# Patch writes paced at one per slot, six shared patch buffers, and a re-ordered start in a convolution kernel that TensorE bounds

## The chip, the cores and the metric

One core of a Trainium2 chip. The metric is the device time of one execution in microseconds (us). The 22 or 23 executions of the kernel before in a set of rounds spread over 0.8 to 1.1% (3105.9 to 3141.0 us at the widest). The record marks every execution here as undisturbed ("fast"). A change counts as faster or slower when it moves the time by over 2%, here 62 us.

## The reference, cut to what matters

For each of 16 images of 256 channels and 28 x 28 pixels: a group normalization, two 3x3 convolutions in which each channel's nine-pixel patch is replaced by a softmax over 16 centroids, each followed by a batch norm, then a squeeze-and-excite gate and two residual additions.

```python
def amm_conv3x3(x, centroids, w_sub, stride=1):
    patches = jax.lax.conv_general_dilated_patches(x, (3, 3), (stride, stride), 'SAME')
    p = patches.reshape(B, C, s, Ho * Wo).transpose(0, 3, 1, 2)
    d = jnp.sum(p * p, axis=-1)[..., None] - 2.0 * jnp.einsum('bncs,cks->bnck', p, centroids) + jnp.sum(centroids * centroids, axis=-1)[None, None]
    attn = jax.nn.softmax(-d, axis=-1)
    lut = jnp.einsum('cks,cso->cko', centroids, w_sub)
    out = jnp.einsum('bnck,cko->bno', attn, lut)
...
v = _gn(x)
out = relu(bn(amm_conv3x3(v, centroids1, wsub1)))
out = se_layer(bn(amm_conv3x3(out, centroids2, wsub2)))
return x + relu(out + v)
```

## The kernel before

The program is a plan of slots. A stage is one layer of one image: two pixel tiles (384 and 400 pixels) times eight groups of channels, 16 units, one per slot. I call a stage of layer 1 "L0" and one of layer 2 "L1"; they alternate, 32 in all, numbered 0 to 31. In each slot TensorE makes one unit's logits (L549) from its patches, ScalarE (ACT) takes the exponential (L607), TensorE makes the numerators (L617), VectorE and GpSimd transpose and divide, and TensorE multiplies with the sub-weights three slots later (L681, "looks").

The patches go through DRAM. Twelve writes per image and layer put the shifted image there, issued from ACT's queue, 588 KB each. Each unit then loads its part with four transfers of about 110 KB from SP's queue. In layer 2 four units of a stage are "maxed": their logits are made six slots early, and their maxima go out to DRAM (`dm<-mt`) and come back (`pm<-dm`) by small transfers, also on ACT's queue.

```python
    def to_pat(l, i, pat):                       # one of 12 patch writes
        ...
        nc.scalar.dma_start(
            view(pat, (ROWS * p0 + 9 * k + 3 * dx) * HW, [[ROWS * HW, n], [HW, 3], [1, HW]]),
            bass.AP(v.tensor, v.offset, [list(v.ap[0]), [W, 3], [1, HW]]),
        )
    ...
    def patches(u):                              # the four loads of a unit
        (px, n), mx = u["px"], u["maxed"]
        tiles = pms if mx else pts               # 2 tiles for maxed units, 4 for others
        pt = tiles[loads[mx] % len(tiles)]
        ...
        for i in range(4):
            nc.sync.dma_start(pt[32 * i : 32 * i + ROWS, :, :n], view(u["pat"], ...))
    ...
        def prep(self, l, pat, t, pace):
            for i, dx in enumerate((0, 2)):
                for k in range(NB):
                    self.at(t + i, REST, shift, l, dx, k)
            for i in range(len(STEPS)):
                self.at(t + i // pace, REST, to_pat, l, i, pat)
    ...
        elif l == 0 and b > 1:
            t0 = t - 2 * NS                      # NS = 16
            plan.at(t0, REST, load_x, b, x[b])
            plan.norm(b, t0 + 3)
            plan.prep(0, pat_of(0, b), t0 + 12, 1)
        if l == 1:
            near = b in (0, B - 1)
            plan.prep(1, pat_of(1, b), t - NS + (LC if near else 0), 3 if near else 2)
```

## Time and profile before

| | kernel before |
|---|---|
| time | 3122.45 us, median of 3 runs (3121.16 to 3123.53) |
| span of the profiled run | 3124.6 us |
| TensorE busy | 2951.3 us, mean granted clock 0.974 |
| up to the first numerators | 51.8 us |
| stage 0, stage 1 | 139.6, 129.6 us |
| 13 full L0 stages (3, 5, ... 27) | 1260.8 us, 93.2 to 102.3 each |
| 14 L1 stages (2, 4, ... 28) | 1233.6 us |
| stages 29 and 30 | 90.0 and 99.1 us |

A stage runs from the first numerators of its first slot to those of the next stage. The last stage and the tail together take 119 to 123 us in all kernels here.

The prediction shows PE's side. The other side, which it did not show, is what SP's queue of patch loads waits for. Columns: total us, times, the longest.

```profile
SPq L536 <- PE pair L549: 661.1, 276, 10.7
SPq L536 <- DMA pat<-im: 318.4, 62, 11.0
SPq L536 <- DMA pat<-side: 298.7, 113, 23.6
SPq L536 <- DMA dm<-mt: 283.2, 66, 11.5
```

The first line is the loads' natural pace: a buffer comes free when the logits that read it are done. The other three are loads that wait for a patch write (`pat`) or for a maximum going out (`dm`). In the steady part they have no tie by data to that transfer: the writes then going out are for a later stage.

### The profile page before, as it was taken

Reading aid. Unit: us, or ns where it says so; the run is one execution under the profiler, and the core shown is the slowest. Engines: PE = TensorE matmul, PEld = TensorE weight load, DVE = VectorE, ACT = ScalarE, POOL = GpSimd, SP = SyncE. Lnnn points to the kernel's source line nnn. Section 1 sums busy time; section 2 is a strip of 40 time slices with the busy share of each in tenths; the row PEclk is TensorE's granted clock in tenths of the full one; section 3 lists DMA queues with packets and bytes.
Section 4 is the critical chain, followed back from the end, with each engine's and each line's share of the span. In section 5 each row is a group of like instructions: output and inputs, shape, how many; then the busy total and the mean of one; then the engine's idle time right before and its main releaser. Section 6 shows DMA issues by size and latency. Waiting matters only on the chain. (4 is left out here: it accounts for less than half of the span.)

```text
span 3124.6 us, 94006 instructions
## 1 busy us (share of the span) xinstructions
PE 2951.3 (94%) x39838; PEld 1167.1 (37%) x39838; DVE 2255.7 (72%) x2756; ACT 1094.0 (35%) x1611; POOL 1504.2 (48%) x2165
## 2 busy tenths in 40 slices
PE   3898999999999999999999999999999999999997
PEld 2432333333333333333333333333333333333333
DVE  3364777787777877768787776868777777777785
ACT  1332343333433334343333433333333333334232
POOL 1343455454545545454555545445554454545344
PEclk9998999999999999999999999999999999999998
DMA  7666666665766666567666656766566666656641
GB/s 209 187 165 147 152 197 172 178 171 149 204 171 196 168 179 161 143 195 185 193 166 169 184 145 194 188 187 157 155 182 166 195 164 174 167 146 196 179 103 50
DMA packets 331901, 530.23 MB, mean 170 GB/s; under 512 B 93664, under 2 KB 251088, under 8 KB 331472
## 3 DMA queue, kind: packets, MB, share of 16 engines
q10 hardware_dynamic: 144000, 244.45, 30.2%
q1 hardware_dynamic: 180560, 241.14, 29.1%
q0 software_dynamic: 6912, 38.54, 3.6%
q8 instruction: 316, 5.18, 0.7%
q14 instruction: 113, 0.93, 0.1%
HBM read 269.96 MB, written 254.05 MB: 168 GB/s over the span
## 5 line engine op out<-in xcount | busy, mean ns | idle before, releaser
L681 PE MATMUL acc<-q,ws 128*128 128x384 f32 (+1 forms) x4096 | 1662.4, 525 | 5.3 <-ACT y L703 5.3
L645 POOL TENSOR_TENSOR k<-nt,rc 128x832 f32<-128x832 f32 (+1 forms) x512 | 804.3, 1571 | 1579.6 <-DVE rc L635 1573.6
L629 DVE STREAM_TRANSPOSE nt<-pair 128x832 f32<-128x832 f32 (+1 forms) x1024 | 978.1, 993 | 765.1 <-PE pair L617 625.9
L607 ACT ACTIVATE e<-pair 128x800 f32<-128x800 f32 (+1 forms) x1024 | 787.2, 821 | 1511.1 <-PE pair L549 1251.5
L681 PEld LDWEIGHTS acc<-q,ws 128*128 128x128 f32 x4096 | 704.9, 191 | 917.0 <-issue 595.1
L617 PE MATMUL pair<-e,cw 32*32 32x384 f32 (+1 forms) x16384 | 601.3, 509 | 60.5 <-ACT e L607 60.1
L663 DVE STREAM_TRANSPOSE q<-k 128x832 f32<-128x832 f32 (+1 forms) x512 | 489.2, 956 | 0.8 <-POOL k L645 0.8
L549 PE MATMUL pair<-pt,wd 19*32 19x384 f32 (+1 forms) x14336 | 439.2, 509 | 22.8 <-DMA pt<-pat 22.5
L635 DVE RECIPROCAL rc<-nt 128x104 f32<-128x104 f32 (+1 forms) x512 | 398.7, 779 | 17.6
L617 PEld LDWEIGHTS pair<-e,cw 32*32 32x32 f32 x16384 | 169.7, 103 | 414.0 <-ACT e L607 382.8
L651 POOL TENSOR_TENSOR tail<-nt,rc 128x104 f32<-128x104 f32 (+1 forms) x512 | 244.8, 478 | 0.0
L681 PE MATMUL acc<-qt,ws 128*128 128x400 f32 (+1 forms) x512 | 221.5, 515 | 0.0
L549 PEld LDWEIGHTS pair<-pt,wd 19*32 19x32 f32 x14336 | 107.1, 103 | 285.1 <-issue 210.1
L657 POOL TENSOR_TENSOR total<-total,nt 128x96 f32<-128x96 f32 (+1 forms) x448 | 200.2, 447 | 0.0
L657 POOL TENSOR_TENSOR total<-total,rc 128x96 f32<-128x96 f32 (+1 forms) x448 | 177.8, 397 | 0.0
L549 PE MATMUL pair<-pm,wd 19*32 19x384 f32 (+3 forms) x4096 | 147.4, 502 | 10.7 <-DMA pm<-pat 10.5
L568 DVE STREAM_TRANSPOSE z<-pair 128x768 f32<-128x768 f32 (+1 forms) x128 | 120.3, 978 | 38.4 <-PE pair L549 38.4
L681 PEld LDWEIGHTS acc<-qt,ws 128*128 128x128 f32 x512 | 91.7, 191 | 102.1 <-issue 53.2
L573 DVE TENSOR_REDUCE mx<-z 128x48 f32<-128x768 f32 (+1 forms) x128 | 120.8, 944 | 0.0
L693 ACT ACTIVATE im<-acc,bnsh,bnsc 128x384 f32<-128x384 f32 (+1 forms) x64 | 43.4, 678 | 154.5 <-PE acc L681 154.5
L703 ACT ACTIVATE y<-acc,bnsh,bnsc 128x384 f32<-128x384 f32 (+1 forms) x64 | 43.4, 678 | 91.6 <-PE acc L681 76.3
L549 PEld LDWEIGHTS pair<-pm,wd 19*32 19x32 f32 (+1 forms) x4096 | 34.4, 103 | 104.5 <-issue 65.4
(105 smaller groups left out, 763.1 us busy)
## 6 DMA issues: line engine op xcount, KB each, us to landing
pat<-side ACTq DMA_DIRECT2D x256, 588.0 KB
pt<-pat SPq DMA_DIRECT2D x896, 112.5 KB
pt<-pat SPq DMA_DIRECT2D x896, 108.0 KB
pat<-im ACTq DMA_DIRECT2D x128, 588.0 KB
xt<-in_x POOLq DMA_DIRECT2D x32, 784.0 KB, 9.7
pm<-pat SPq DMA_DIRECT2D x128, 112.5 KB
pm<-pat SPq DMA_DIRECT2D x128, 108.0 KB
out_dram<-y POOLq DMA_DIRECT2D x16, 784.0 KB, 4.5
```

What stands on the lines that cost most here:

```text
L549: nc.tensor.matmul(ps[t // 2][c : c + 32, t % 2, :n], lhsT=wd[l][32 * i : 32 * i + rows, 4 * u["m"] + t, :], rhs=u["pt"][32 * i : 32 * i + ...
L568: nc.vector.transpose(z[:, : 64 * nb].rearrange("p (t m) -> p t m", t=2), ps[:, :, : 32 * nb])
L573: nc.vector.tensor_reduce(u["mx"][:, 2 * v : 2 * v + 2].rearrange("p t (j b) -> p t b j", j=2)[:, :, :nb], u["z"].pop(0)[:, : 64 * nb].rea ...
L607: nc.scalar.activation(e[:, :, :n], ps[:, :, :n], AF.Exp, scale=2.0)
L617: nc.tensor.matmul(u["nm"][t // 2][32 * i : 32 * i + 32, t % 2, :n], lhsT=cw[l][c : c + 32, 4 * u["m"] + t, :], rhs=es[t // 2][c : c + 32, ...
L629: nc.vector.transpose(nt[:, :nb, 2 * v : 2 * v + 2].rearrange("p b t r -> p t b r"), ps[:, :, : 32 * nb].rearrange("p t (b r) -> p t b r", ...
L635: nc.vector.reciprocal(rc[:, : 8 * nb], u["nt"][:, :, SUM])
L645: nc.gpsimd.tensor_tensor(q[:, :nb].rearrange("p b (a s) -> p (b a) s", s=8), nt[:, :, :8], rc.unsqueeze(2).to_broadcast([P, 8 * nb, 8]), ...
L651: nc.gpsimd.tensor_tensor(tails[key][:, :nb, 8 * (m % 4) : 8 * (m % 4) + 8], nt[:, :, 8].rearrange("p (b a) -> p b a", a=8), rc.rearrange( ...
L657: nc.gpsimd.tensor_add(t[:, : 8 * nb], t[:, : 8 * nb], v)
L663: nc.vector.transpose(q[:, :, : 32 * nb].rearrange("p h (b r) -> p h b r", r=32), u.pop("k")[:, :nb].rearrange("p b (h r) -> p h b r", h=2),)
L681: nc.tensor.matmul(accs[key][:, :n], lhsT=ws[l][:, 2 * m + h if h < 2 else 2 * NQ + m // 4, o * P : (o + 1) * P], rhs=u["q"][h][:, :n], st ...
```

## The change

Its intent: take the patch writes of layer 2 from two per slot at the start of an L0 stage to one per slot in L1 stages, so that they stop holding up ACT; share six patch buffers among all units; move the normalization to where the memory is quieter (DMA share 0.58 in the L1 stage that the prediction shows, 0.70 in the L0 stage after it); and shorten the start, by writing and using the first pixel tile first.

```diff
-    pts = [const.tile([P, 4, 400], F32, name=f"pt{i}") for i in range(4)]
-    pms = [const.tile([P, 4, 400], F32, name=f"pm{i}") for i in range(2)]
+    pts = [const.tile([P, 4, 400], F32, name=f"pt{i}") for i in range(6)]
...
         def emit(self):
+            free = [-99] * len(pts)
+            for slot, last, u in sorted(self.loads, key=lambda v: v[:2]):
+                tile = free.index(min(free))
+                assert free[tile] <= slot
+                free[tile] = last
+                self.at(slot, LOAD, patches, u, tile)
...
-                        at(a - self.lead + 1, REST, patches, u)
+                        self.loads.append((a - self.lead, s, u))
...
-        def prep(self, l, pat, t, pace):
+        def prep(self, l, pat, t):
+            for i, dx in enumerate((0, 2)):
+                for k in range(NB):
+                    self.at(t + 4 * i + 2 + k, REST, shift, l, dx, k)
+            for i in range(len(STEPS)):
+                self.at(t + i, REST, to_pat, l, i, pat)
+
+        def prep_near(self, l, pat, t, slots, t2, slots2):     # images 0 and 15
...
+                self.at(t + i * slots // len(STEPS), REST, to_pat, l, i, pat, *PXT[0])
+                self.at(t2 + i * slots2 // len(STEPS), REST, to_pat, l, i, pat, *PXT[1])
...
+        if l == 0 and b >= 1:
+            n0 = -3 if b == 1 else t - 2 * NS - 3
+            plan.at(n0 - 2, REST, load_x, b, x[b])
+            plan.norm(b, n0)
+            plan.prep(0, pat_of(0, b), {1: 1, 2: 32, 3: 56}.get(b, t - 2 * NS + 3))
         if l == 1:
-            plan.prep(1, pat_of(1, b), t - NS + (LC if near else 0), 3 if near else 2)
+            if b in (0, B - 1):
+                t0 = t - NS + LC
+                plan.prep_near(1, pat_of(1, b), t0, 4, t0 + 4, 8)
+            else:
+                plan.prep(1, pat_of(1, b), 44 if b == 1 else t - 2 * NS + LC + 1)
...
-    for i in range(NLT * P // PART):
-        plan.at(i // 3, REST, sort_ws1, i)
+    n1 = NLT * P // PART
+    for i in range(n1):
+        if i < 2:
+            plan.at(-6, REST, load_part, ws1, i)
+            plan.at(-1, REST, sort_ws1, i)
+        else:
+            plan.at((i - 2) * 3 // 4 - 1, REST, load_part, ws1, i)
+            plan.at((i - 2) * 3 // 4, (LOOK_A, LOOK_B)[i % 2], sort_ws1, i)
```

Cut: the second pixel tile of image 0 is written in slots 0 to 3, the second layer's sub-weights are loaded a slot before their sort, the set-up of its codes moves from slot 20 to 15, the squares of the codes go to a function of their own, one of three copies of a sort goes to VectorE, the norm takes six slots instead of eight, and three placing moves per slot replace four.

More of the change, by code (lines that the diff above doesn't have):

```diff
@@ L150 @@
     load_x(0, x[0])
-    pts = [const.tile([P, 4, 400], F32, name=f"pt{i}") for i in range(4)]
-    pms = [const.tile([P, 4, 400], F32, name=f"pm{i}") for i in range(2)]
-    for t in pts + pms:
+    pts = [const.tile([P, 4, 400], F32, name=f"pt{i}") for i in range(6)]
+    for t in pts:
         nc.sync.dma_start(t[ONE::32], view(consts, 0, [[0, 4], [0, 4], [1, 400]]))
@@ L295, with load_part @@
     PART = 384
-    def part_of(ap, i):
+    parts = {}
+    def load_part(ap, i):
         t = tpool.tile([P, 832], F32, tag="z", name="part")[:, : NB * PART].rearrange("p (b m) -> p b m", b=NB)
         nc.sync.dma_start(t, ap[:, i * PART : (i + 1) * PART].rearrange("(b p) m -> p b m", p=P))
-        return t
+        parts[i] = t
     def sort_ws1(i):
-        t = part_of(ws1, i)
+        t = parts.pop(i)
         for j in range(PART // P):
@@ L310, in sort_ws1 @@
                 )
-            nc.scalar.copy(ws[0][:, i * PART // P + j], ps[:, :C])
+            w = ws[0][:, i * PART // P + j]
+            if j == 1:
+                nc.vector.tensor_copy(w, ps[:, :C])
+            else:
+                nc.scalar.copy(w, ps[:, :C])
     d_c2 = [dram.tile([C, K * 9], F32, name=f"dc2{i}") for i in range(2)]
@@ L337, in sort_ws2 @@
     def sort_ws2(i):
-        t = part_of(wsub2, i)
+        t = parts.pop(i)
         ps = pair()
@@ L374, in place_tail, with square_codes @@
         )
+    squares = []
+    def square_codes(l):
+        wf = wd[l].rearrange("p t m -> p (t m)")
+        for c0 in range(0, NT * 32, 384):
+            n = min(384, NT * 32 - c0)
+            sq = tpool.tile([P, 832], F32, tag="z", name="sq")[:, :n]
+            nc.gpsimd.tensor_tensor(sq, wf[:, c0 : c0 + n], wf[:, c0 : c0 + n], ALU.mult)
+            squares.append((c0, n, sq))
     def setup_codes(l):
         wf = wd[l].rearrange("p t m -> p (t m)")
-        for c0 in range(0, NT * 32, 256):
-            sq = tpool.tile([P, 832], F32, tag="z", name="sq")
-            nc.gpsimd.tensor_tensor(sq[:, :256], wf[:, c0 : c0 + 256], wf[:, c0 : c0 + 256], ALU.mult)
+        for c0, n, sq in squares:
             ps = bank()
-            nc.tensor.matmul(ps[:, :256], lhsT=nhalf_sb, rhs=sq[:, :256], start=True, stop=True)
-            nc.vector.tensor_add(wf[:, c0 : c0 + 256], wf[:, c0 : c0 + 256], ps[:, :256])
+            nc.tensor.matmul(ps[:, :n], lhsT=nhalf_sb, rhs=sq, start=True, stop=True)
+            nc.vector.tensor_add(wf[:, c0 : c0 + n], wf[:, c0 : c0 + n], ps[:, :n])
+        squares.clear()
         nc.vector.tensor_add(wd[l], wd[l], mones_sb[:, l].unsqueeze(1).to_broadcast([P, NT, 32]))
@@ L448, with to_pat @@
     STEPS = [(dx, k, h) for dx in (1, 0, 2) for k in range(NB) for h in range(2)]
-    def to_pat(l, i, pat):
+    def to_pat(l, i, pat, px=0, n=HW):
         dx, k, h = STEPS[i]
-        p0, n = P // 2 * h, P // 2
-        v = (ims[l] if dx == 1 else sides[dx])[p0 : p0 + n, k]
+        p0, m = P // 2 * h, P // 2
+        v = (ims[l] if dx == 1 else sides[dx])[p0 : p0 + m, k, px:]
         nc.scalar.dma_start(
-            view(pat, (ROWS * p0 + 9 * k + 3 * dx) * HW, [[ROWS * HW, n], [HW, 3], [1, HW]]),
-            bass.AP(v.tensor, v.offset, [list(v.ap[0]), [W, 3], [1, HW]]),
+            view(pat, (ROWS * p0 + 9 * k + 3 * dx) * HW + px, [[ROWS * HW, m], [HW, 3], [1, n]]),
+            bass.AP(v.tensor, v.offset, [list(v.ap[0]), [W, 3], [1, n]]),
         )
@@ L524, in store, with patches @@
             d.pop(b)
-    loads = {True: 0, False: 0}
-    def patches(u):
-        (px, n), mx = u["px"], u["maxed"]
-        tiles = pms if mx else pts
-        pt = tiles[loads[mx] % len(tiles)]
-        u["mx"] = mxs[loads[mx] % 2]
-        loads[mx] += 1
+    maxed = [0]
+    def patches(u, tile):
+        px, n = u["px"]
+        pt = pts[tile]
+        if u["maxed"]:
+            u["mx"] = mxs[maxed[0] % 2]
+            maxed[0] += 1
         for i in range(4):
@@ L710 @@
     LOOKS = [(m, o, h) for m in range(NQ) for o in range(2) for h in range(3 if m % 4 == 3 else 2)]
-    LOGITS, EXP, LOOK_A, NUM, TURN, SMALL, LOOK_B, MAX, LOOK_C, TURN_BACK, REST = range(11)
+    LOGITS, EXP, LOOK_A, NUM, TURN, SMALL, LOOK_B, MAX, LOOK_C, TURN_BACK, LOAD, REST = range(12)
     class Plan:
@@ L722, in __init__ @@
             self.tiles = []
+            self.loads = []
         def at(self, slot, pos, f, *a):
@@ L761, in stage @@
                     else:
-                        at(s - self.lead, REST, patches, u)
+                        self.loads.append((s - self.lead, s, u))
                     at(s, LOGITS, b_logits, u)
@@ L775, in prep @@
             for i in range(len(STEPS)):
-                self.at(t + i // pace, REST, to_pat, l, i, pat)
+                self.at(t + i * slots // len(STEPS), REST, to_pat, l, i, pat, *PXT[0])
+                self.at(t2 + i * slots2 // len(STEPS), REST, to_pat, l, i, pat, *PXT[1])
         def norm(self, b, t):
             self.at(t, REST, gn_stats, b, 0)
-            self.at(t + 2, REST, gn_stats, b, 1)
-            self.at(t + 4, SMALL, gn_mean, b)
-            self.at(t + 5, SMALL, gn_var, b)
-            self.at(t + 6, REST, gn_apply, b, 0)
-            self.at(t + 7, REST, gn_apply, b, 1)
+            self.at(t + 1, REST, gn_stats, b, 1)
+            self.at(t + 2, SMALL, gn_mean, b)
+            self.at(t + 3, SMALL, gn_var, b)
+            self.at(t + 4, REST, gn_apply, b, 0)
+            self.at(t + 5, REST, gn_apply, b, 1)
         def close(self, b, ob, te, pace):
@@ L815 @@
             shift(0, dx, k)
-        to_pat(0, i, d_pat[0])
+        to_pat(0, i, d_pat[0], *PXT[0])
+    square_codes(0)
     setup_codes(0)
@@ L825 @@
         plan.stage(l, b, pat_of(l, b), t, () if l == 0 else MAXED)
-        if l == 0 and b == 1:
-            plan.at(-4, REST, load_x, b, x[b])
-            plan.norm(b, -3)
-            plan.prep(0, pat_of(0, b), 5, 2)
-        elif l == 0 and b > 1:
-            t0 = t - 2 * NS
-            plan.at(t0, REST, load_x, b, x[b])
-            plan.norm(b, t0 + 3)
-            plan.prep(0, pat_of(0, b), t0 + 12, 1)
-        if l == 1:
-            near = b in (0, B - 1)
-            plan.prep(1, pat_of(1, b), t - NS + (LC if near else 0), 3 if near else 2)
+        if l == 0 and b >= 1:
[3 more added lines that the diff above has]
+            plan.prep(0, pat_of(0, b), {1: 1, 2: 32, 3: 56}.get(b, t - 2 * NS + 3))
+        if l == 1:
+            if b in (0, B - 1):
[3 more added lines that the diff above has]
+                plan.prep(1, pat_of(1, b), 44 if b == 1 else t - 2 * NS + LC + 1)
             plan.at(t + NS, REST, load_x, b, x[b])
             plan.close(b, out[b], t + NS + LC, 1 if b < B - 2 else 2)
-    for i in range(NLT * P // PART):
-        plan.at(i // 3, REST, sort_ws1, i)
+    for i in range(len(STEPS)):
+        plan.at(i // 3, REST, to_pat, 0, i, d_pat[0], *PXT[1])
+    n1 = NLT * P // PART
[3 more added lines that the diff above has]
+            plan.at(-1, REST, sort_ws1, i)
+        else:
+            plan.at((i - 2) * 3 // 4 - 1, REST, load_part, ws1, i)
+            plan.at((i - 2) * 3 // 4, (LOOK_A, LOOK_B)[i % 2], sort_ws1, i)
     plan.at(3, REST, sort_c2)
     for i in range(9 * C // PART):
+        plan.at(3 + i, REST, load_part, wsub2, i)
         plan.at(4 + i, REST, sort_ws2, i)
@@ L850 @@
     for i, (f, *a) in enumerate(moves):
-        plan.at(6 + i // 4, REST, f, *a)
-    plan.at(20, REST, setup_codes, 1)
+        plan.at(6 + i // 3, REST, f, *a)
+    plan.at(14, REST, square_codes, 1)
+    plan.at(15, REST, setup_codes, 1)
     plan.emit()
@@ L872 @@
             plan.norm("g", 0)
-            plan.prep(0, d_pat[0], 8, 1)
+            plan.prep(0, d_pat[0], 8)
             s0 = 32
             plan.stage(0, "g", d_pat[0], s0, range(NQ))
-            plan.prep(1, d_pat[2], s0 + plan.end, 1)
+            plan.prep(1, d_pat[2], s0 + plan.end)
             s1 = s0 + plan.end + 24
```

## The prediction

> **What bounds the kernel now.** I read the page first. TensorE (PE) is the bound, with VectorE far behind, and the chain of waits that ended last is almost all matmuls (L681, L617, L549).
>
> ```profile
> PE 2951.3 (94%) x39838; PEld 1167.1 (37%) x39838; DVE 2255.7 (72%) x2756; ACT 1094.0 (35%) x1611; POOL 1504.2 (48%) x2165
> PEclk9998999999999999999999999999999999999998
> L617 PE MATMUL pair<-e,cw 32*32 32x384 f32 (+1 forms) x16384 | 601.3, 509 | 60.5 <-ACT e L607 60.1
> L549 PE MATMUL pair<-pt,wd 19*32 19x384 f32 (+1 forms) x14336 | 439.2, 509 | 22.8 <-DMA pt<-pat 22.5
> ```
>
> The change removes no matmul of the steady loop, so it can win only PE's 173 us of idle (3124.6 less 2951.3) and the half-clock stretches inside the busy figure (mean clock 0.974: 0.026 x 3124.6 = 81 us). The groups say that PE idles mostly for ACT's exponentials (L607) and for patches.
>
> To see where, I counted the groups of 32 records of L617 in PE's timeline: 512, one per slot, 16 per stage (layer 1: "L0", layer 2: "L1"). Then I asked for the engines' busy time between stage borders. Columns: stretch, its length, busy us of PE, PEld, DVE, ACT, POOL, PE clock, DMA share, GB/s.
>
> ```profile
> 51.80:191.40 139.60, 120.77 (x1278) 58.11 (x1278) 57.50 (x66) 43.82 (x69) 44.28 (x69) 0.96 0.65 164
> 191.40:321.00 129.60, 109.51 (x1243) 40.15 (x1242) 69.58 (x87) 34.90 (x48) 47.58 (x76) 0.87 0.67 162
> ...
> 2164.30:2252.20 87.90, 87.64 (x1235) 34.52 (x1234) 68.45 (x81) 28.06 (x40) 41.35 (x58) 1.00 0.58 146
> 2252.20:2354.50 102.30, 96.31 (x1247) 37.10 (x1246) 71.68 (x88) 39.34 (x61) 52.27 (x78) 0.92 0.70 192
> ...
> 2815.40:2905.40 90.00, 88.72 (x1243) 34.59 (x1242) 69.30 (x82) 34.62 (x53) 49.49 (x70) 1.00 0.65 185
> 2905.40:3004.50 99.10, 92.66 (x1298) 35.45 (x1297) 74.14 (x89) 30.42 (x43) 40.65 (x57) 0.97 0.58 155
> 3004.50:3100.10 95.60, 90.29 (x1219) 36.71 (x1219) 71.11 (x88) 31.39 (x50) 47.34 (x64) 0.96 0.30 76
> ```
>
> The reader is to see that an L1 stage (third line) takes 88 us with PE full and the clock at 1.00, while the L0 stage after it has nearly as many matmul records and takes 102. All 14 L1 stages lie between 87.4 and 88.9; the 13 full L0 stages lie between 93.2 and 102.3 and add up to 1260.8. The fifth line is the one L0 stage without normalization and without layer-1 patches to write: 90.0. The first two stages cost 269 us.
>
> Inside such an L0 stage there is one gap, always 21 us after its start:
>
> ```profile
> 2271.53 1.56 PE L681 MATMUL acc<-q,ws 128*128 128x384 f32 x4
> 2276.85 2.23 PE L617 MATMUL pair<-e,cw 32*32 32x384 f32 x32 [3.76 <-ACT e L607]
> ...
> 2279.95 2.93 PE L681 MATMUL acc<-q,ws 128*128 128x384 f32 x4
> ```
> ```profile
> 2273.47 2.41 ACTq L454 DMA_DIRECT2D pat<-side  x2
> 2275.99 1.51 ACT L607 ACTIVATE e<-pair 128x768 f32<-128x768 f32 x2 [6.44 <-DMA pt<-pat]
> ```
>
> PE waits 3.76 us for the exponential, which stands in ACT's queue behind two patch writes (L454); ACT idled 6.44 us there, and what ended it was a DMA. The issues themselves take about 0.6 us each. In the trace the ACT and SP DMAs share eight semaphores in turn, and an issue first waits until the earlier transfer on its semaphore has landed; so eight transfers are in flight at most, and a slow one blocks the engine queue that wants to reuse its semaphore. Reading landing times as the last semaphore count before its next use, a patch write lands after 6.3 to 8.3 us (medians by slot) where two are issued per slot (L0 slots 0 to 5), and after 4.8 to 6.2 us where one is. DMA runs at 0.98 and 278 GB/s in the 18 us before this gap. After it the matmuls of L681 take 2.93 us per four, not 1.56: the clock record has half speed for 13.65 us there.
>
> [...] gaps of 2.04, 2.45 and 2.97 us leave the clock at 1, those of 3.4 to 4.5 us are followed by half speed in lengths that are multiples of 3.41 us (3.41 to 13.65), though 2.36 to 2.89 were enough in three stages too.
>
> **The change part by part.**
>
> *Steady loop: the patch writes.* Layer 2's 12 writes per image (588 KB each) go from two per slot in L0 slots 0 to 5 to one per slot in L1 slots 4 to 15; layer 1's 12 go to L0 slots 3 to 14, from L0 12 to L1 7. The image load for the norm moves from L0 slot 0, where it met the 784 KB reload for the residual, to L1 slot 11. Bytes asked for in L0 slots 0 to 5 now: 12 x 588 KB + 2 x 784 KB + 6 x 441 KB of patches = 11.3 MB in some 33 us, 340 GB/s, more than the 278 seen. After: (588 + 441) KB per 5.6 us slot = 184 GB/s, plus one 784 KB transfer now and then. The old kernel already shows one write per slot in an L1 stage (slots 0 to 7), and it has no stall there (PE 87.64 of 87.90). So I expect the gap gone and the clock at 1. The full L0 stages should come to 89.2 (102.3 less 6.0 of idle and 6.8 of clock loss gives 89.5; the others give 87 to 90) plus about 1 us of small waits that stay, above all the 0.84 us wait of the second norm matmul for GpSimd, since norm still leaves one slot between the two. 13 x 90.2 = 1172.6, so **-88 us**. L1 stages have four writes more than before: 0.
>
> *Six shared buffers.* Now a load for a "maxed" unit is issued in the slot whose logits free its tile, SP in order behind it. With six shared tiles I count at most five live (L1, slots 3 and 7 of eight), so tiles come free earlier. Removes the "pm" waits (10.7 us over the kernel, some of it in the start): **-3 us**, included in the next terms and in slack.
>
> *Prologue to the first L617 (51.8 us).* The 12 writes of image 0 go first for pixels 0 to 383 alone, half the bytes: 3.5 rather than 7.1 MB. Written from 17.4 to about 43 us now, they were moving near 270 GB/s; half ends near 31 to 34, held by ACT's four shifts (0.82 us each) and 12 issues. But two 384 KB loads of sub-weights and their sorts come in front of the first logits (24 records[...], some 8 us after the permutation at 35 us). I take the first L617 at 46: **-6 us**.
>
> *Stage 0 (139.6).* Idle 18.8 and clock loss 5.1. Two of six sorts leave it (36 records took 8.04 us warm, so 12 take 2.7 each: -5), the code setup enters (+2.5). The loads of sub-weights come a slot earlier, which removes waits of 7.5, 3.5 and 4.0 us; in the first slots PE still waits for ACT and DVE, and three half-size writes per slot are new. I keep about 6 us of idle and 2 of clock: 139.6 - 13 (idle) - 3 (clock) - 2.5 (work) = 121: **-19**.
>
> *Stage 1 (129.6).* Idle 20.1, clock loss 13.9. The 3.95 us wait for squares plus 3.8 of setup leaves (squares a slot ahead, in stage 0's last slots). The 9.84 us wait came where three whole writes per slot, four placing moves and four loads met; now half-size writes, three moves. Still ten transfers per slot for eight semaphores, so I keep half of the rest: 129.6 - 8 - 16 = 106: **-24**.
>
> *Last image (99.1).* Idle 6.4, clock loss 3.4; three half-size writes per slot instead of three whole: 92: **-7**. The last stage (95.6, a 5.31 us wait for the store of the previous image) and the 24 us tail are untouched: 0.
>
> Sum: -88 - 6 - 19 - 24 - 7 = -144, near 2978. I add 7 us for stalls I don't see: **2985 us**.
>
> **The rivals.** (1) *The stall moves instead of vanishing.* L1 stages now hold 12 writes and 16 small transfers of maxima, whose issues also block ACT (ACT's waits for "dm<-mt" come to 118.5 us, hidden today because ACT is busy 28 of 88 us). If a third of the gap came back per period: 13 x 2 to 3 us, so 3010 to 3025. Against it: the old L1 slots 0 to 7 with the same mix are clean. (2) *The gap is not the DMA at all but the norm's work on ACT and DVE in L0.* Then it follows the norm to its new slots and the steady part wins little: 3060 to 3080 from the start alone. Against it: the L0 stage without norm still shows a 1.0 us gap at the same place, and what ended ACT's wait is a DMA. (3) *VectorE becomes the bound* once PE is full: it has 71.7 us of work per L0 stage and 68.4 per L1, and gains 2 to 3 in L1, so it stays under 85% of 88. Unlikely. (4) *The start gets worse*: many small issues on ACT's queue block exponentials in slots 0 to 3. That takes away 10 to 25 us, giving 3000 to 3010.
>
> **Range and chances.** The steady part alone, at 88 us, is 2.8% of 3122, over the 2% limit (62 us) without any gain in the start; to miss 2% both it and the start must fail. Low end: start without any stall and L0 at 89: 2950. High end: rivals 1 and 4 together: 3030. Faster by over 2%: 0.95; within 2%: 0.04; slower: 0.01.
>
> **What would show it.** Right: L0 and L1 stages both near 88 to 90 us, PE clock 1.00 from stage 2 on, ACT's waits ended by "DMA pt<-pat" in the steady part (64.8 us between 600 and 3040) gone, patch writes landing in under 6.5 us, first L617 near 46, stage 1 near 106. Wrong: an L1 stage over 91 us with ACT waiting for a DMA (rival 1), a gap at the norm's new slots (rival 2), or a first two stages still over 250 us (rival 4).

## The result

The changed kernel took 3109.32 us (median of 4 runs, 3104.46 to 3118.07); before, on the same chip, 3122.23 (3121.16 to 3123.53). The ratio is 0.9962, 95% interval 0.9939 to 0.9984. Ratios in this text are the record's, of fast runs of the same rounds, so not quite the ratio of the medians quoted. The time is the same within 2%; the prediction was 2985.

By the same count of stages, in the profiled run of each:

| stretch | before | after | moved | predicted |
|---|---|---|---|---|
| to the first numerators | 51.8 | 54.8 | +3.0 | -6 |
| stage 0 | 139.6 | 124.9 | -14.7 | -19 |
| stage 1 | 129.6 | 125.9 | -3.7 | -24 |
| 13 L0 stages | 1260.8 | 1257.8 | -3.0 | -88 |
| 14 L1 stages | 1233.6 | 1235.4 | +1.8 | 0 |
| stage 29 | 90.0 | 86.7 | -3.3 | 0 |
| stage 30 | 99.1 | 97.9 | -1.2 | -7 |
| span | 3124.6 | 3103.0 | -21.6 | -144, given as -137 |

The page of the changed kernel, busy times and clock:

```profile
PE 2966.8 (96%) x39834; PEld 1165.8 (38%) x39834; DVE 2254.3 (73%) x2760; ACT 1094.8 (35%) x1605; POOL 1506.4 (49%) x2163
PEclk8998999999999999999999999999999999999998
```

PE's idle fell from 173 to 136 us, but its busy time rose by 15.5 us with the same matmuls. Half-clock stretches stayed: from stage 2 through stage 30 the clock record has 95.6 us at 0.5 before (11 stretches) and 92.2 after (13). The two groups that answer to L617 and L549 of before:

```profile
L563 PE MATMUL pair<-pt,wd 19*32 19x384 f32 (+2 forms) x18432 | 626.5, 509 | 60.5 <-DMA pt<-pat 58.6
L631 PE MATMUL pair<-e,cw 32*32 32x384 f32 (+1 forms) x16384 | 585.9, 507 | 14.5 <-ACT e L621 13.3
```

The wait has changed its name. PE used to idle 60 us for ACT's exponential; that is now 13. It now idles 59 us for patch loads, which was 22.5. The stretches of an L1, an L0 and an L1 stage (20, 21, 22), then the last part of stage 21 in four pieces. Columns as in the prediction.

```profile
1969.05:2057.53 88.48, 88.27 (x1237) 34.73 (x1236) 70.62 (x87) 30.58 (x44) 42.43 (x60) 1.00 0.67 175
2057.53:2155.18 97.65, 93.78 (x1245) 35.69 (x1244) 69.16 (x82) 37.06 (x56) 51.16 (x77) 0.97 0.72 176
2155.18:2243.08 87.90, 87.90 (x1237) 34.74 (x1237) 70.70 (x87) 30.59 (x44) 42.55 (x60) 1.00 0.67 172
...
2117.00:2131.00 14.00, 13.82 (x183) 4.99 (x181) 10.98 (x14) 4.67 (x7) 8.60 (x12) 1.00 0.86 233
2131.00:2137.50 6.50, 6.21 (x89) 2.32 (x104) 4.19 (x5) 1.56 (x2) 2.82 (x4) 1.00 0.74 190
2137.50:2147.00 9.50, 6.59 (x69) 1.68 (x38) 3.65 (x5) 0.25 (x1) 2.80 (x4) 0.87 0.68 163
2147.00:2155.00 8.00, 8.00 (x76) 2.75 (x75) 3.56 (x4) 2.49 (x4) 0.70 (x1) 0.73 0.62 137
```

The L1 stages are full. Nearly all of stage 21's loss lies in its last 18 us: a gap, then a clock of 0.87 and 0.73. The DMA engines are not full there (0.74, 0.68), but busier in the 14 us before (0.86, 233 GB/s); before the old gap they were at 0.98. PE's timeline of that place:

```profile
2138.89 0.83 PE L695 MATMUL acc<-qt,ws 128*128 128x400 f32 x2
2142.63 4.11 PE L563 MATMUL pair<-pt,wd 19*32 19x400 f32 x32 [2.91 <-DMA pt<-pat]
2146.67 3.04 PE L695 MATMUL acc<-q,ws 128*128 128x400 f32 x4
```

PE waits 2.91 us for the patches of the stage's last unit, and then runs at half speed (3.04 us for four looks, 1.61 before the gap). The 2.91 us understate the stall: the unit's four loads landed one by one (2142.50 to 2145.07, table below), and until the last of them only 6 of the 32 logit matmuls are on record, in what the profile counts as busy time. Over the 13 stages the medians of slots 3 and 4, where the old gap and its half clock were, fell from 8.66 and 8.85 us to 5.62 and 5.43, and that of slot 14 rose from 8.40 to 14.94: what one place won, the other lost. ACT's and SP's queues at the same time, from three answers of the timeline:

```profile
2129.89 1.78 ACTq L602 DMA_DIRECT2D dm<-mt  x2
2131.71 0.61 ACTq L468 DMA_DIRECT2D pat<-side  x1
...
2128.27 2.65 SPq L550 DMA_DIRECT2D pt<-pat  x3
...
2137.67 3.35 SPq L550 DMA_DIRECT2D pt<-pat  x4
```

SP issues a load until 2130.9 and none until 2137.67. SP's waits there, and over the whole program:

```profile
SPq L550 <- DMA pat<-side: 6.7, 1, 6.7
...
SPq L550 <- DMA pat<-side: 650.6, 180, 14.0
SPq L550 <- DMA pat<-im: 404.4, 63, 15.1
SPq L550 <- DMA pt<-pat: 378.1, 491, 4.6
SPq L550 <- DMA dm<-mt: 304.6, 55, 21.4
SPq L550 <- PE pair L563: 123.6, 223, 4.0
```

Against before: waits for a free buffer fell from 661.1 to 123.6 us, so the six shared buffers did what they were for. Waits for patch writes rose from 617.1 (318.4 + 298.7) to 1055.0 (404.4 + 650.6). One write holds SP for 6.7 us in stage 21. Such a sum is no cost by itself: l0_early below has SP wait 929.2 us for writes (367.4 + 561.8) and is faster than both kernels. What matters is which load waits, and how soon it is due.

Why does a load wait for a write? Here are the issues of that stretch with the semaphore that each transfer counts up, and its landing, read as that semaphore's last count before its next use:

```
us        queue  transfer   semaphore  lands
2131.71   ACT    write T10  115        2137.61     the eleventh of layer 1's 12 writes
2136.03   ACT    pt<-dm     112        2138.31
2136.64   ACT    pt<-dm     114        2138.86
2137.24   ACT    write T11  116        2142.40
2137.67   SP     pt<-pat    115        2142.50     first load of the last unit
2138.03   SP     pt<-pat    108        2143.34
2138.61   SP     pt<-pat    110        2144.11
2140.18   SP     pt<-pat    111        2145.07
```

The load at 2137.67 uses semaphore 115, on which T10 landed only at 2137.61. In the traces of the two kernels the issues of both queues use eight semaphores, 108 and 110 to 116, and fit one common order that takes them in strict turn (all 2834 steps in the changed kernel, all 2798 in the one before). No transfer is seen to go out before the one ahead on its semaphore has landed: the full count stands before the next issue in 2822 of 2827 cases (2786 of 2791 before), and in the other five some counts are missing from the record altogether. That order is not the plan's order of slots: this load stands in the plan's slot 12 and T10 in slot 13, but in it T10 stands eight places before the load. So the load, and every load behind it on SP, waits for T10 to land, and lands itself 4.8 us later, too late for its logits. In the kernel before, the same order held ACT. At the gap that the prediction shows, one write stood behind a write of the slot before (issued at 2265.18, landed at 2273.45), and the next behind a load issued at 2263.70 that took 11.6 us to land. The pacing changed who stands behind whom.

### The profile page after: what moved, and what is told of

The parts are those of the page before. It is cut to its first block, busy times and chain, and to the rows that moved or that the text cites. A ratio compares the mean times of both kernels' runs of the same rounds, so it can differ in the third digit from the quotient of the medians.

```text
span 3103.0 us, 94273 instructions
## 1 busy us (share of the span) xinstructions
PE 2966.8 (96%) x39834; PEld 1165.8 (38%) x39834; DVE 2254.3 (73%) x2760; ACT 1094.8 (35%) x1605; POOL 1506.4 (49%) x2163
## 4 chain that ended last, share of the span: by engine, by line
PE 76%; DMA 10%; DVE 5%; POOL 3%; issue 2%; ACT 2%; ACTq 1%; SPq 0%; POOLq 0%; DVEq 0%
PE acc L695 45%; PE pair L631 15%; PE pair L563 15%; DMA pt<-pat 6%; DMA pat<-side 3%; DVE nt L643 2%; POOL k L659 1%; DVE rc L649 1%; ACT e L621 1%; DVE q L677 1%; POOL total L671 1%; DMA pat<-im 1%; ACTq L468 1%; PE pair L324 1%; DVE gn_st L417 0%
## 5 line engine op out<-in xcount | busy, mean ns | idle before, releaser
L563 PE MATMUL pair<-pt,wd 19*32 19x384 f32 (+2 forms) x18432 | 626.5, 509 | 60.5 <-DMA pt<-pat 58.6
L631 PE MATMUL pair<-e,cw 32*32 32x384 f32 (+1 forms) x16384 | 585.9, 507 | 14.5 <-ACT e L621 13.3
L563 PEld LDWEIGHTS pair<-pt,wd 19*32 19x32 f32 (+1 forms) x18432 | 149.3, 103 | 440.6 <-issue 265.6
L525 DVE SCALAR_TENSOR_TENSOR y<-xt,gn_rstd,y 128x392 f32<-128x392 f32 x64 | 71.2, 1116 | 1.2 <-ACT y L519 1.2
L533 POOL TENSOR_TENSOR y<-y,xt 128x392 f32<-128x392 f32 x64 | 64.8, 1015 | 11.0 <-ACT y L529 11.0
```

The lines of the kernel that those rows point to most:

```text
L563: nc.tensor.matmul(ps[t // 2][c : c + 32, t % 2, :n], lhsT=wd[l][32 * i : 32 * i + rows, 4 * u["m"] + t, :], rhs=u["pt"][32 * i : 32 * i + ...
L631: nc.tensor.matmul(u["nm"][t // 2][32 * i : 32 * i + 32, t % 2, :n], lhsT=cw[l][c : c + 32, 4 * u["m"] + t, :], rhs=es[t // 2][c : c + 32, ...
```

## The experiments

The theory (A): the lost time is set by which transfer stands eight places ahead of an urgent one in that order. The rivals: (B) the writes and loads together ask for too much bandwidth at that place; (C) the store of the previous image, which falls there, is what slows them. Stage sums below are from each run's one profiled execution; gaps are PE's idle time in a slot, as a mean over the 13 L0 stages.

| run | median us | ratio to before, 95% | 13 L0 | 14 L1 | stage 1 | stage 30 |
|---|---|---|---|---|---|---|
| before | 3120.5 to 3123.7 | 1 | 1260.8 | 1233.6 | 129.6 | 99.1 |
| the change | 3109.32 | 0.9962, 0.9939 to 0.9984 | 1257.8 | 1235.4 | 125.9 | 97.9 |
| t_on_sp | 3074.21 | 0.9854, 0.9816 to 0.9891 | 1206.7 | 1261.8 | 108.4 | 97.6 |
| t_on_pool | 3107.09 | 0.9957, 0.9944 to 0.9970 | 1260.5 | 1257.1 | 104.1 | 90.0 |
| half_bytes | 3046.88 | 0.9762, 0.9722 to 0.9803 | 1206.7 | 1231.0 | 123.6 | 97.9 |
| l0_early | 3027.50 | 0.9694, 0.9646 to 0.9741 | 1157.3 | 1258.7 | 125.9 | 96.2 |
| store_late | 3098.36 | 0.9907, 0.9877 to 0.9936 | 1255.8 | 1235.2 | 126.9 | 96.8 |
| four_two | 3105.13 | 0.9937, 0.9919 to 0.9955 | 1252.8 | 1242.6 | 130.7 | 91.7 |
| old_pacing | 3074.92 | 0.9838, 0.9791 to 0.9884 | 1246.0 | 1225.7 | 124.1 | 90.3 |
| early_near_pool | 3000.04 | 0.9594, 0.9546 to 0.9642 | 1155.8 | 1258.0 | 111.0 | 89.8 |
| third_load | 3102.63 | 0.9953, 0.9940 to 0.9966 | 1256.3 | 1234.0 | 125.0 | 96.0 |
| best | 2990.34 | 0.9600, 0.9563 to 0.9637 | 1153.3 | 1252.0 | 106.3 | 90.0 |

All gave correct results but half_bytes, which is wrong on purpose. By the 2% rule l0_early, early_near_pool and best are faster than the kernel before, half_bytes and old_pacing are unclear, and the others are the same.

**t_on_sp: the patch writes on SP's queue.**

```diff
 def to_pat(...):
-        nc.scalar.dma_start(
+        nc.sync.dma_start(
```

> The changed kernel with one edit: the patch writes are issued from SP's queue instead of ACT's. Theory A (semaphore order: the load for the sixteenth unit of a layer-1 stage reuses the semaphore of a patch write that ACT issues only two slots before the unit is due): with writes and loads in one queue no load of a layer-1 stage stands behind a write younger than five slots before it is due, so the stall at 81 to 85 us of each layer-1 stage goes, those stages come to 88 to 90 us, and the whole to 3010 to 3040 us. Theory B (bandwidth: a 588 KB write and 441 KB of loads per slot are too much for the DMA engines): same bytes in the same slots, so the same stall, 3100 to 3120 us. Theory C (the 784 KB store of the previous image in slot 11 delays the loads): the same, 3100 to 3120 us.

Measured: 3074.21 us (3065.57 to 3079.89), which neither theory's range has. The L0 stages lost 3.9 us each ((1257.8 - 1206.7) / 13), and their gap in slot 14 fell from 2.89 to 0.76 us; but the L1 stages gained 1.9 each. That is a third to a half of the gain that A gave. The stall is smaller, but it stays, with another holder: in stage 21 SP stands 20.4 us for a maximum, which goes out at 2097.23, when its data is ready, and lands at 2099.54. The last unit's four loads follow at 2100.63 to 2104.09, at the start of the slot in which they are due. In the 22 us before, the DMA engines were at 0.26 and moved 72 GB/s (`--windows 2077.38:2099.50`). Loads that go out late while the DMA engines are at 0.26 speak against B: what held them was their place in the order. The new order has stalls of its own in the L1 stages, which I did not follow up.

**t_on_pool: the patch writes on GpSimd's queue, out of the rotation.**

```diff
-        nc.scalar.dma_start(
+        nc.gpsimd.dma_start(
```

> The changed kernel with the patch writes issued from GpSimd's queue, which has eight semaphores of its own. Theory A: loads wait only for loads and maxima, the stall goes: 3010 to 3045 us, unless GpSimd's time[...] (24 writes per image, some 0.9 us each as for its image loads) delays its scaling. Theories B and C: same bytes at the same time, 3100 to 3120 us.

Measured: 3107.09 us (3101.0 to 3123.19, 20 runs): a miss for the number that A gave. By the time alone this speaks for B. In the traces of the two kernels GpSimd's 48 transfers count up eight other semaphores, 100 to 107, six each; here SP's waits for patch writes fell from 1055.0 to 60.3 us. The trace shows what held the loads: SP's waits in 2105 to 2142 of its stage 21, then SP's issues in that stretch.

```profile
SPq L550 <- DMA dm<-mt: 24.7, 2, 22.2
...
2111.03 30.74 SPq L550 DMA_DIRECT2D pt<-pat  x6
```

SP waits 22.2 us in one piece for a maximum going out. Without the writes in the rotation, the place eight before SP's next load is held by `dm<-mt`, which is issued at 2131.65, when its data is ready, and lands at 2135.33; the load is issued at 2135.39. It is the last one of the unit before. The last unit's first load stands behind the second maximum, which takes 6.1 us to land (2132.05 to 2138.12), and goes out at 2138.18. The gap in slot 14 is 2.71 us, but by other holders. I had worked out what would leave the rotation, and not what would then stand in its place. In stages 1 and 30 the writes' leaving does help (104.1 and 90.0 us).

**half_bytes: the same order, but every write from image 4 on only half as wide.** Wrong result on purpose (relative error 0.484).

```diff
-                self.at(t + i, REST, to_pat, l, i, pat)
+                self.at(t + i, REST, to_pat, l, i, pat, 0, n)     # n = HW // 2 from image 4 on
```

> Wrong result on purpose: from image 4 on each patch write moves only the left half of its columns, from ACT's queue in the same slots; the order in which the semaphores are handed out around the sixteenth unit is the same as in the changed kernel. Theory A: the write still goes out only in slot 13, and lands perhaps 2 us sooner of 6, so the stall shrinks by 2 to 3 us of its 7 per stage: 3070 to 3095 us. Theory B: with 294 KB instead of 588 KB per slot the stall goes: 3010 to 3030 us. Theory C: the store still meets the loads, with less beside it: 3060 to 3110 us.

Measured: 3046.88 us, between the numbers of A and B. T10 still stands before the same load, and lands 3.6 us after its issue instead of 5.9; the stage then ends with a shorter wait (timeline of its stage 21):

```profile
2101.88 1.86 PE L563 MATMUL pair<-pt,wd 19*32 19x400 f32 x28 [0.64 <-DMA pt<-pat]
```

A smaller write shortens the wait under both theories; this run alone does not tell them apart.

**l0_early: the same transfers, the same queues and bytes; norm and layer-1 writes three slots earlier from image 4 on.**

```diff
-            plan.at(n0 - 2, REST, load_x, b, x[b])
-            plan.norm(b, n0)
-            plan.prep(0, pat_of(0, b), {1: 1, 2: 32, 3: 56}.get(b, t - 2 * NS + 3))
+            plan.at(n0 - 2 - (3 if b > 3 else 0), REST, load_x, b, x[b])
+            plan.norm(b, n0 - (3 if b > 3 else 0))
+            plan.prep(0, pat_of(0, b), {1: 1, 2: 32, 3: 56}.get(b, t - 2 * NS))
```

> The changed kernel with the norm and the patch writes of layer 1 three slots earlier (slots 0 to 11 of the layer-1 stage instead of 3 to 14), from image 4 on. Theory A: the youngest write that a load stands behind is three slots old instead of two; the stall at the end of the stage goes, 3020 to 3060 us. Theory B: the same bytes per slot, the backlog grows over the same twelve slots and the stall moves three slots forward: 3100 to 3120 us. Theory C: the store in slot 11 no longer meets writes behind it: part of the stall goes, 3060 to 3100 us.

Measured: 3027.50 us (3013.88 to 3034.51), as A predicted. Its stages 20 to 22:

```profile
1918.12:2008.37 90.25, 88.64 (x1239) 34.97 (x1238) 70.65 (x87) 32.71 (x47) 43.96 (x66) 1.00 0.65 170
2008.37:2096.21 87.84, 87.84 (x1244) 34.69 (x1243) 69.23 (x82) 35.09 (x53) 49.53 (x70) 1.00 0.72 194
2096.21:2186.46 90.25, 88.85 (x1240) 35.10 (x1239) 70.64 (x87) 32.70 (x47) 43.96 (x66) 1.00 0.65 169
```

The L0 stage has no idle time and full clock while it moves 194 GB/s, where the change moved 176 and stalled. The two move the same bytes (17.0 and 17.2 MB, rate times length), so the stage as a whole does not ask for too much. PE's last logits of that stage:

```profile
2087.05 0.83 PE L695 MATMUL acc<-qt,ws 128*128 128x400 f32 x2
2087.81 1.99 PE L563 MATMUL pair<-pt,wd 19*32 19x400 f32 x32
2089.74 1.61 PE L695 MATMUL acc<-q,ws 128*128 128x400 f32 x4
```

They are just in time: 1.99 us instead of 0.95, with no gap and no half clock. The loads before the stage's end stand behind the two `dm<-mt` here, as in t_on_pool. But the first lands 3.2 us after its issue (2079.16 to 2082.34), and the second one 3.0 us after its own, where t_on_pool had 3.7 and 6.1, with writes going on beside them. So the order names the holder, and by these times it held longer with writes beside it: B alone is not the cause, but it is a factor in A's sum. The L1 stages pay 1.7 us each ((1258.7 - 1235.4) / 14).

**store_late: the store of the previous image four slots later.**

```diff
-            self.at(te + 5 + 3 // pace, REST, store, b, ob)
+            self.at(te + 5 + 3 // pace + (4 if pace == 1 else 0), REST, store, b, ob)
```

> The changed kernel with the 784 KB store of each finished image four slots later (slot 15 of the layer-1 stage instead of 11). The order of the semaphores is the same. Theory A (semaphore order): the stall in slot 14 stays, 3095 to 3120 us. Theory C (the store delays the loads of slots 12 to 14): the stall goes, 3020 to 3070 us.

Measured: 3098.36 us; the gap in slot 14 stays, at 2.82 us. C is out.

**four_two: the buffers undone (four and two, maxed loads one slot later), the pacing kept.**

```diff
-                tile = free.index(min(free))
-                assert free[tile] <= slot
-                free[tile] = last
-                self.at(slot, LOAD, patches, u, tile)
+                mx = u["maxed"]
+                tile = 4 + self.n[mx] % 2 if mx else self.n[mx] % 4
+                self.n[mx] += 1
+                self.at(slot, REST if mx else LOAD, patches, u, tile)
...
-                        self.loads.append((a - self.lead, s, u))
+                        self.loads.append((a - self.lead + 1, s, u))
```

> The changed kernel with the buffers undone: four for ordinary units, two for maxed ones, whose loads go out a slot later. In the built order of semaphores the sixteenth unit's load then stands behind the tenth write (slot 12, three slots before it is due) instead of the eleventh (slot 13). Theory A: a smaller stall, 3045 to 3095 us, so that the six buffers made it worse. Rival D (the six buffers are what lets SP run ahead, and without them loads come later): 3110 to 3150 us.

Measured: 3105.13 us, a miss: I expected a gain because the last unit's load no longer stands behind T10 in that order. In its trace another load is held: that of a maxed unit whose logits are due in slot 14 waits for a maximum that goes out at 2138.71 and lands at 2142.76, and is issued at 2142.78. I had followed one load and not all that are due in the slot. With the new pacing the buffers make no difference that shows (3105 and 3109 us).

**old_pacing: the old pacing of writes and norm in the steady part, the new buffers and the new start kept.** Cut from the diff: `prep` takes a pace again, and the image load goes out a slot earlier.

```diff
-            n0 = -3 if b == 1 else t - 2 * NS - 3
+            n0 = -3 if b == 1 else t - 2 * NS - 3 if b < 4 else t - 2 * NS + 3
...
-            plan.prep(0, pat_of(0, b), {1: 1, 2: 32, 3: 56}.get(b, t - 2 * NS + 3))
+            plan.prep(0, pat_of(0, b), {1: 1, 2: 32, 3: 56}.get(b, t - 2 * NS + 12))
...
-                plan.prep(1, pat_of(1, b), 44 if b == 1 else t - 2 * NS + LC + 1)
+                plan.prep(1, pat_of(1, b), 44 if b == 1 else t - NS, 1 if b == 1 else 2)   # pace 2
```

> The changed kernel with the steady pacing undone: from image 4 on the norm and the writes of layer 1, and from image 2 on those of layer 2, in the slots of the kernel before, two layer-2 writes per slot; buffers and start as changed. Theory A: a layer-2 write again reuses the semaphore of the write issued one slot before, which takes 8 us to land, so ACT blocks in slot 3 as before: layer-1 stages 94 to 99 us, 3095 to 3120 us. Rival D (the six buffers remove the old gap by themselves): 3020 to 3070 us.

Measured: 3074.92 us (3071.16 to 3083.44), between the ranges of A and D. The old gap for the exponential is back, 2.97 us per L0 stage in slot 3 (timeline of stage 21), and the L0 stages come to 95.8 us each, within A's 94 to 99:

```profile
2071.31 1.58 PE L631 MATMUL pair<-e,cw 32*32 32x384 f32 x32 [2.68 <-ACT e L621]
```

Yet this kernel is 34 us faster than the change (3109.32 - 3074.92). The profiled run, the slowest of its four, is 21.0 us shorter than the change's (3103.0 - 3082.0): -11.8 us in the L0 stages, -9.7 in the L1 stages and -7.6 in stage 30, against +6.5 in stage 29. So the new pacing, from which the prediction took 88 of its 144 us, cost time on top of the change's other parts. The six buffers do not remove the old gap, so D is out.

**early_near_pool: l0_early, with the half-size writes of images 0 and 15 on GpSimd's queue.**

```diff
+        q = nc.scalar if n == HW else nc.gpsimd
-        nc.scalar.dma_start(
+        q.dma_start(
```

> A candidate for the best: the norm and layer-1 writes three slots earlier from image 4 on, and the half-size writes (image 0, layer-2's first and last image) issued from GpSimd's queue. Theory A: the steady part stays as with the earlier slots alone (3027 us), and the start and the stage before the last one lose the waits of ACT and SP on each other, as they did with all writes on GpSimd (22 us less in the first two stages, 6 in that stage): 2990 to 3015 us. Theory B: bandwidth binds in those stages, so no gain there: 3020 to 3035 us.

Measured: 3000.04 us. Stage 1 came to 111.0 us and stage 30 to 89.8, but the first numerators moved from 54.4 to 59.5 us, since image 0's first writes went to that queue too.

**third_load: one load of the start earlier.** The first numerators had come later than before the change. PE's timeline of the changed kernel:

```profile
38.90 6.90 PE L309 MATMUL pair<-sort_sb,part 128*128 128x256 f32 x24 [0.25 <-ACT gn_gm L425]
45.73 0.93 PE L563 MATMUL pair<-pt,wd 19*32 19x384 f32 x32
49.40 5.46 PE L309 MATMUL pair<-sort_sb,part 128*128 128x256 f32 x12 [2.74 <-DMA part<-in_ws]
54.79 1.23 PE L631 MATMUL pair<-e,cw 32*32 32x384 f32 x32
```

The first logits come at 45.73 us, but a third sort stands between them and the numerators, and its load was issued at 41.68 us behind twelve patch loads.

```diff
-            plan.at((i - 2) * 3 // 4 - 1, REST, load_part, ws1, i)
+            plan.at(-6 if i == 2 else (i - 2) * 3 // 4 - 1, REST, load_part, ws1, i)
```

> The change with one load earlier: the third part of the first layer's sub-weights is asked for with the first two (ahead of the twelve first patch loads) instead of behind them. In the change PE waits 2.74 us for that part in slot 0 and then sorts it in 5.46 us, and the first numerators come at 54.8 us. Theory (the start was mis-sized because the third sort, and the load behind which it stands, lie ahead of the first numerators): the wait goes, the sort takes about 3 us, and the first numerators come at 49.5 to 51.5 us, as early as or earlier than in the kernel before (51.8); the whole time falls by 3 to 5 us, too little for the timing to show well (ratio to the change's own 0.996 of 0.9945 to 0.9955). Rival (the exponential of slot 0 or the second sort sets that point, not the load): first numerators stay at 54 to 56 us. The steady part, with its gap of about 3 us in slot 14 of each layer-1 stage, must not change under either.

The same place in this run:

```profile
45.72 0.93 PE L563 MATMUL pair<-pt,wd 19*32 19x384 f32 x32
46.57 2.98 PE L309 MATMUL pair<-sort_sb,part 128*128 128x256 f32 x12
49.48 0.93 PE L631 MATMUL pair<-e,cw 32*32 32x384 f32 x32
```

Measured: the wait is gone, the sort takes 2.98 us instead of 5.46 at half clock, and the first numerators come at 49.5 us, at the theory's early end. Not all of the 5.3 us is the edit's. In store_late, whose start is that of the change, the wait for the same part was 1.71 us, the clock stayed full and the first numerators came at 52.0; in the change the clock's fall to half, at 48.70 by its record, added to the wait. Stage 0 grew from 124.9 to 128.7 us: the two together take 178.2 us instead of 179.7. The point was moved, and most of the gain was given back in the next slots. The time (3102.63 us, ratio 0.9953) does not stand clear of the change's (0.9962, 0.9939 to 0.9984).

**best: l0_early, only layer 2's half-size writes on GpSimd's queue, and the third load early.**

```diff
+        q = nc.gpsimd if l == 1 and n < HW else nc.scalar     # all of layer 2's half-size writes
```

> Norm and layer-1 patch writes three slots earlier, only the second layer's half-size writes of the first tile on GpSimd's queue (the first image's own writes stay on ACT's), and the third part of sub-weights loaded with the first two. Against the version with all half-size writes on GpSimd's queue (3000.0 us, first numerators at 59.5): the first numerators come back to 50 to 52 us, stage 1 stays near 111 and stage 30 near 90, steady layer-1 stages stay at 87.8 to 90 with no gap in slot 14. Semaphore order as the cause: 2990 to 2996 us, ratio 0.957 to 0.960. If the gain of that version in stage 1 had come from taking the first image's writes off ACT's queue rather than the second layer's, stage 1 goes back to about 125 and the time to 3005 to 3010.

One correction to the text on record: the condition takes all half-size writes of layer 2 for images 0 and 15, both tiles. Measured: 2990.34 us (2989.23 to 2993.5), ratio 0.9600: 4.0% faster than the kernel before and the best here. First numerators at 50.7 us, stage 1 at 106.3, stage 30 at 90.0: as A expected, with stage 1 some 5 us better. So stage 1's gain comes with layer 2's writes leaving ACT's queue and its rotation, not with the first image's. Its busy times and clock:

```profile
PE 2893.7 (97%) x39834; PEld 1154.2 (39%) x39834; DVE 2254.2 (75%) x2760; ACT 1096.5 (37%) x1605; POOL 1534.4 (51%) x2211
PEclk7999999999999999999999999999999999999998
```

PE's idle is 94.6 us (2988.3 - 2893.7), and its busy time is 73 us under the change's, with the same matmuls. What is left in the steady part is mainly 0.9 us (mean of 14) in slot 10 of L1 stages. Lines of ACT and of PE there:

```profile
2129.80 1.16 ACTq L609 DMA_DIRECT2D pt<-dm  x2
2131.01 0.67 ACT L718 ACTIVATE y<-acc,bnsh,bnsc 128x384 f32<-128x384 f32 x1 [3.61 <-DMA pt<-dm]
...
2133.27 1.63 PE L632 MATMUL pair<-e,cw 32*32 32x400 f32 x32 [1.29 <-ACT e L622]
```

ACT's queue waits for a maximum to land (6.4 us after its issue) before it can issue its return, and the work behind it comes late.

## Why the prediction was wrong

**The step that failed** is the one on the steady loop: "The old kernel already shows one write per slot in an L1 stage (slots 0 to 7), and it has no stall there ... So I expect the gap gone and the clock at 1", worth -88 us. It got -3.0. The diagnosis of the old gap held: it is gone from slot 3, comes back there in old_pacing, and waits of ACT's exponential for "DMA pt<-pat" fell from 71.1 to 24.3 us. The step priced a rate of transfers (184 GB/s instead of 340). What decided in the traces was the order in which eight semaphores go round both queues, and when the transfer ahead lands (in stage 21 T10 landed at 2137.61, and the load behind it went out at 2137.67). The prediction had named those eight semaphores, and that a slow transfer blocks the queue that reuses its semaphore; but in its price it used only the rate. It did not ask, for each urgent load of the new order, what stands eight places ahead. A write that lands in 5.9 us, within the 6.5 that it had asked for, still makes a load late that is due in the slot after the write's. The run l0_early shows the rest: with the same transfers three slots earlier, the L0 stages come to 1157.3 us, under the predicted 1172.6, though the L1 stages then take 25 us more than before (1258.7 against 1233.6, predicted 0). A slip beside this: the 6.8 us of clock loss in the 102.3 us stage count only the first of two half-clock stretches there (13.65 and 3.41 us).

**Rival 1** ("The stall moves instead of vanishing") came true, with the wrong place and size. It put the return in L1 stages, by the maxima blocking ACT, and at a third. The stall came back in L0 stages, by a write blocking SP, and whole: 3.00 us of gap per L0 stage before (slot 3), 2.89 after (slot 14). What it described did show at a small size in the runs with the norm and the layer-1 writes three slots earlier: 0.9 us per L1 stage in best, by ACT's wait for a maximum.

**Six buffers.** Right that tiles come free earlier (waits 661.1 to 123.6 us). Wrong that this removes waits on balance: SP ran on to the next wait, that for a write or for another load (253.8 to 378.1 us).

**Start.** First numerators: 54.8 us, predicted 46. The prediction counted 24 sort records ahead of the first logits, which did come at 45.73, but overlooked the third sort between logits and numerators. With that mended they come at 49.5. Stage 0: -14.7 for -19, about right. Rival 4 (small issues on ACT's queue hold up exponentials in slots 0 to 3) came true here: PE waits 8.8 us for exponentials in stage 0, against 4.2 before, and the two long waits (4.50 us to 72.11, 3.80 to 84.12) end when ACT has come through its half-size writes (68.02 to 71.20 and 78.74 to 83.16 in its timeline). Its sign, first two stages over 250 us, was met (250.8). In best these waits are still 10.7 us. Of the 34 us by which the start fell short of its price, 20 lie in stage 1.

**Stage 1.** -3.7 for -24. The wait for squares left as said, but loads of weights and patches stood behind half-size writes (SP's waits for writes there: 22.7 and 4.4 us with patch loads, 8.7 with loads of weights). Two of PE's waits there, 4.92 and 4.46 us, in the changed kernel:

```profile
248.09 4.64 PE L563 MATMUL pair<-pt,wd 19*32 19x400 f32 x32 [4.92 <-DMA pt<-pat]
270.44 3.81 PE L563 MATMUL pair<-pt,wd 19*32 19x400 f32 x32 [4.46 <-DMA pt<-pat]
```

With layer 2's half-size writes out of the rotation the stage took 106.3 us in best; the prediction was 106. Stage 30 the same: 97.9 in the change, 90.0 with those writes out, predicted 92.

**Rivals 2 and 3** fell: only 0.35 us of gap per L0 stage in slot 0, where one of the norm's new slots lies, and VectorE is at 73%.

Read against best, three of the prediction's prices look near: 13 L0 and 14 L1 stages together -89.1 us (predicted -88), stage 1 -23.3 (-24), stage 30 -9.1 (-7). The first is luck: the L0 stages gave -107.5 (-88) and the L1 stages +18.4 (0), two misses that cancel. The start stayed short: -1.1 us (-6) to the first numerators and -9.6 (-19) in stage 0. And best is a kernel that had to be found; the change was not free of these stalls. The range was too narrow for what was known: nothing in it allowed for the gap coming back whole.

**What stays open.** Why old_pacing gains 34 us over the change in L1 stages too is not followed up, nor the 1.9 us that t_on_sp costs per L1 stage. No run changes the order of the semaphores and nothing else: t_on_sp and l0_early also move transfers in time, and so the traffic at that place. In slots 12 and 13 of stage 21 the DMA engines were at 0.91 in the change, 0.28 in t_on_sp and 0.60 in l0_early. Theory A rests on these runs together with the issues read in the traces; how much of a holder's time to land is traffic is not separated. Why the build places T10 ahead of a load of an earlier slot was not looked into.

## What to carry to other kernels

When two queues share a few semaphores in turn, as ACT's and SP's share eight in these traces, list for every load that is due soon which transfer stands that many places ahead of it, and when that one can go out and land; a rate of bytes did not tell here (the DMA engines were at 0.72 in the stage 21 that stalled and in the one of l0_early that did not). After each such change make the list again for all urgent loads: taking one holder away puts the next in its place, as three runs here showed (t_on_sp, t_on_pool, four_two). And count a stall as gone only when the busy engine's own gaps are gone, in every slot: here slot 3 lost its gap and slot 14 got one. Sums of a queue's waits do not tell this either: in best SP still waits 872.9 us for patch writes (536.3 + 336.6), more than in the kernel before (617.1).

## What the traces show of queues, semaphores and clock

- The choice of queue weighed: the same writes from SP instead of ACT took the kernel from 3109 to 3074 us, and layer 2's half-size writes from GpSimd brought stage 1 from 125.9 us (l0_early) to 106.3 (best). In these traces the wait for a semaphore comes with the issue: SP's waits for patch writes came to 1055.0 us in the change, the longest 15.1.
- The price of eight semaphores for two queues: in stage 21 a load waited 6.7 us for an unrelated write eight places ahead, and everything behind it on that queue waited too.
- The length of PE's gap did not settle here whether the clock fell to half. In the change's start the clock record falls to half at 48.70 us, 2.0 us into a gap of 2.74 (twelve sort records then took 5.46 us, and 2.98 without the gap), and at 1775.85, 1.6 us into a gap of 2.04; in the kernel before, a gap of 2.04 us (to 798.95) left it full. After the 2.91 us gap of stage 21 it falls only at 2144.49, 1.9 us after the gap's end, while loads still came in one by one.
